# Two factors moved ahead of four transposes, and one difference moved behind two sums, on VectorE's queue in a two-layer graph attention kernel

## The chip, the cores and the metric

The kernel runs on one core of a Trainium2 chip. A core has TensorE (PE, matrix products into PSUM), VectorE (DVE), ScalarE (ACT), GpSimd (POOL, unused here but for some constants) and SyncE (SP), which issues all DMAs. Each engine works through its own queue of instructions and waits on semaphores for the others. The metric is the device time of one execution in microseconds (us), taken as the median of several runs.

## The reference

32 graphs ("elements") of 512 nodes with 512 features, and two layers, all in float32. Layer 0 is attention with 8 heads, in which the adjacency multiplies the exponentials, and a layer norm; layer 1 is a graph attention whose logits are a sum of two vectors:

```python
q, k, v = heads(x @ Wq.T + bq), heads(x @ Wk.T + bk), heads(x @ Wv.T + bv)
logits = einsum('bhqd,bhkd->bhqk', q, k) / sqrt(64) + log(clip(adj, 1e-8, None))
out = einsum('bhqk,bhkd->bhqd', softmax(logits), v) @ Wo.T + bo
x = layer_norm(x + out)
f = x @ fc_w.T + fc_b
m = (f @ q_w + q_b) + (f @ k_w + k_b).T + (1 - adj) * -1e9
out = softmax(leaky_relu(m)) @ f + x
```

## The kernel before

The elements go through a software pipeline written out by hand. For element b the kernel runs layer 0 of b beside layer 1 of element b - 2 and the joining work of element b - 1. The order of instructions on every engine is the order in which the Python functions issue them; no scheduler changes it. Elements 2 to 30 go through `first_two` (head pairs 0 and 1) and `second_two` (head pairs 2 and 3), thus 29 times. Elements 0 and 1 go through `slot`, and element 31 through `joining_slot` and `slot`. `joining_slot` has its own copy of the sequence that the change touches.

Products of 512 x 512 matrices are done as seven products of quarters with sums and differences (Strassen's scheme in Winograd's form). In layer 1 the product z = n^T e^T (n: the normalised features, e: the softmax weights) is done by `seven_z`. Its two operands are first made on VectorE. The weights of element b - 2 are "spread" by 16 DMAs of 64 KB (`spread_blocks`, L148) that are issued at the end of `second_two` of the element before; `eT` then turns them in place with four transposes of 32 x 32 blocks (L576). Sums and differences of quarters follow. The lines of `seven_z` that matter here, A for quarters of n, E for quarters of the turned weights:

```python
left = {1: A["11"], 2: A["12"], 3: A["12"], 4: A["22"], 5: s1, 6: A["11"], 7: A["21"]}
right = {1: E["11"], 2: E["21"], 3: E["22"], 4: E["21"], 5: t1, 6: E["11"], 7: E["12"]}
def before1():                             # extra[1]: L1073, L1074
    sub(t1, E["12"], E["11"])
    sub(A["21"], A["11"], A["21"])
def after0():                              # extra[2]: L1077, L1078
    sub(E["11"], E["22"], t1)
    sub(A["11"], s1, A["11"])
def after1():                              # extra[3]: L1081
    sub(E["12"], E["22"], E["12"])
```

`extra[0]` (L1070) forms s1, `extra[4]` (L1084, L1085) comes ahead of the fourth product, `extra[5]` (L1088) and `extra[6]` (L1091) add results. On TensorE `zs[0]` is products one and five (16 matmuls each), `zs[1]` six and two, `zs[2]` seven and three, `zs[3]` four. All run through the helper `halves` (L213) into three banks of PSUM, mx, my and mz, whose roles rotate from element to element. ScalarE copies results out (L1052, L1053, L1058, L1059, L1067). Product six reads what L1077 and L1078 write; both of these overwrite an operand of product one.

Ahead of z, `eight_scores` runs the scores of two head pairs (L852 on TensorE) and ScalarE's exponentials (L859, L861) into eight tiles `at`. `factor(b, p, kc)` (L887, VectorE) multiplies such a tile by the adjacency tile cT. The factored tiles are read by the value products (L913), which come on TensorE after z. `scaled` (L468) multiplies n by gamma for the residual, `turn_a` (L598) turns two rows of blocks of cT in place, and `divided` (L949 to L959) inverts sums that have come back through DRAM and sends the reciprocals by DMA to the tile R, which `scale` (L968) reads.

Of the kernel before, what the change touches and what calls it, by code (L numbers as in the profile page):

```python
# [30 lines left out]
def kernel(  # L31
# [280 lines left out]
    def transpose_units(src, dst, psum, evict, name):  # L312

        units = []
        for i in range(4):
            def unit(i=i):
                pt = psum.tile([P, 512], FP, tag="m", name=f"pt_{name}_{i}")
                for c in range(4):
                    nc.tensor.transpose(pt[:, ts(c, P)], src[:, c, ts(i, P)], ident)
                evict(dst[:, i, :], pt)  # L320
            units.append(unit)
        return units
# [144 lines left out]
    def scaled(s, cs):  # L467
        nc.vector.tensor_mul(s["yb"][:, cs, :], s["n"][:, cs, :], over(K["gamma"], cs))  # L468
# [39 lines left out]
    def fast(ctx):  # L508
# [43 lines left out]
        def load_n(b):  # L552
            s = S[b]
            if b > 0:
                tag = "xT" if b == B - 1 else "n"
                s["n"] = act.tile([P, NC, D], FP, tag=tag, name=f"n_{b}")
                load_b(s["n"], x[b])
# [16 lines left out]
        def transposes(dst, src):  # L574
            return [
                lambda c=c: nc.vector.transpose(dst[:, c, :], src[:, c, :]) for c in range(4)  # L576
            ]
# [18 lines left out]
        def turn_a(kcs):  # L596
            for kc in kcs:
                nc.vector.transpose(cT[:, kc, :], cT[:, kc, :])  # L598
# [230 lines left out]
        def long_banks(b):  # L829
            return lambda: [  # L830
                lone[i].rearrange("p (n f) -> p n f", n=KH) for i in (2, 0, 1)
            ]
# [51 lines left out]
        def factor(b, p, kc):  # L884

            at = S[b]["at", p, kc]
            nc.vector.scalar_tensor_tensor(  # L887
                at, cT[:, kc, :].unsqueeze(1).to_broadcast([P, 2, N]), ADJ_MIN, at,
                ALU.max, ALU.mult,
            )  # L890

        def both(b, p):
            run(values(b, p))
# [9 lines left out]
        def values(b, p):  # L903
            s = S[b]
            s.setdefault("oT", [None] * NPAIR)

            def part(half):
                if half == 0:
                    s["po", p] = ps_o.tile([P, N], FP, tag="po", name=f"po_{b}_{p}")
                for kc in (2 * half, 2 * half + 1):  # L910
                    for j in range(2):
                        h = 2 * p + j
                        nc.tensor.matmul(  # L913
                            s["po", p][j * DK : (j + 1) * DK, :],
                            s["v"][h // 4][:, kc, ts(h % 4, DK)],
                            s["at", p, kc][:, j, :],
                            start=(kc == 0), stop=(kc == NC - 1),
                        )
                if half == 1:
                    s["oT"][p] = act.tile([P, N], FP, tag="oT", name=f"oT_{b}_{p}", bufs=6)  # L920
                    nc.scalar.copy(s["oT"][p], s["po", p])  # L921
            return [lambda: part(0), lambda: part(1)]

        def divide(b, p):


            s = S[b]
            ps = lone[0]
            for h in range(4):
                nc.tensor.matmul(  # L930
                    ps[h * BL : (h + 1) * BL, :], ones[:, :BL], s["as", p + h // 2][:, h % 2, :],
                    start=True, stop=True,
                )
            s["R", p] = act.tile([P, 2, N], FP, tag="R", name=f"R_{b}_{p}")
            r = s["R", p][:, 0, :]
            nc.scalar.copy(r, ps)
            m = 4 * N // P
            d0 = dram.tile([4, N], FP, tag="d0", name=f"d0_{b}_{p}")
            nc.sync.dma_start(out=d0, in_=r.rearrange("(h r) n -> h r n", r=BL)[:, 0, :])
            c = small.tile([P, 2, m], FP, tag="c", name=f"c_{b}_{p}")  # L940
            nc.sync.dma_start(out=c[:, 0, :], in_=d0.rearrange("h (a m) -> (h a) m", m=m))
            s["c", p] = c

        def divided(b, p):
            s = S[b]
            c = s["c", p]
            m = 4 * N // P
            i = 2 * b + p // 2
            nc.vector.tensor_scalar(c[:, 1, :], c[:, 0, :], SUM_MAX, None, ALU.is_le)  # L949
            nc.vector.scalar_tensor_tensor(  # L950
                c[:, 1, :], c[:, 0, :], SUM_MIN, c[:, 1, :], ALU.is_ge, ALU.mult,
                accum_out=seen[:, i : i + 1],
            )
            nc.vector.reciprocal(c[:, 0, :], c[:, 0, :])
            d1 = dram.tile([P, m], FP, tag="d1", name=f"d1_{b}_{p}")
            nc.sync.dma_start(out=d1, in_=c[:, 0, :])
            d1 = d1.rearrange("(k j a) m -> j k (a m)", k=2, j=2)
            for j in range(2):
                nc.sync.dma_start(  # L959
                    out=s["R", p][j * DK : (j + 1) * DK, :, :],  # L960
                    in_=d1[j].unsqueeze(0).to_broadcast([DK, 2, N]),
                )

        def scale(b, p):
            s = S[b]
            for k in range(2):
                oT = s["oT"][p + k]
                nc.vector.tensor_mul(oT, oT, s["R", p][:, k, :])  # L968
# [127 lines left out]
        def eT(b):  # L1096
            s = S[b]
            if b >= B - 2:
                t = io.tile([P, NC, N], FP, tag="x", name=f"eT_{b}")
                s["eT"] = t.rearrange("p t (c n) -> p t c n", c=NC)  # L1100
                return transpose_units(s["e"], t, ps_m, nc.scalar.copy, f"e_{b}")
            s["eT"] = s["eP"].rearrange("p c (t n) -> p t c n", t=NC)
            return transposes(s["eP"], s["eP"])
# [46 lines left out]
        def new_yb(b):  # L1150
            S[b]["yb"] = act.tile([P, NC, D], FP, tag="yb", name=f"yb_{b}")
# [144 lines left out]
        def run(units):  # L1296
            for u in units:
                u()
# [173 lines left out]
        def eight_scores(b, ps):  # L1472

            n = 0
            for p in ps:
                for kc in range(NC):
                    score(b, p, kc, n % 3 == 0)
                    n += 1

        def first_two(b):  # L1480

            last, nxt = b - 1, b + 1
            if b == 2:
                run(values(last, 3))
                run(seven_qk(b, 1))
                scale(last, 0)
            divide(last, 2)
            eight_scores(b, (0, 1))  # L1490
            new_yb(b - 2)
            scaled(S[b - 2], slice(0, KH))
            zs, extra = seven_z(b - 2)
            extra[0]()
            run(eT(b - 2))
            extra[1]()
            extra[3]()
            factor(b, 0, 0)
            zs[0]()
            extra[2]()  # L1500
            factor(b, 0, 1)
            scaled(S[b - 2], slice(KH, NC))
            turn_a((2, 3))
            zs[1]()
            extra[4]()
            factor(b, 0, 2)
            zs[2]()
            extra[5]()
            divided(last, 2)
            factor(b, 0, 3)  # L1510
            zs[3]()
            extra[6]()
            load_n(last)
            load_x(nxt)
            factor(b, 1, 0)
            factor(b, 1, 1)
            factor(b, 1, 2)
            factor(b, 1, 3)
            first_difference(last, third)
            wos, wo_adds = seven_wo(last, long_banks(last))  # L1520
            wos[0]()
            both(b, 0)
            next_qk = seven_qk(b, 2)
            next_qk[0]()
            both(b, 1)
            run(sums_in_place(b, 0))
            scale(last, 2)
            first_sum(last)
            run(next_qk[1:4])
            run(sums_in_place(b, 1))  # L1530
            run(next_qk[4:])
            next_qk = seven_qk(b, 3)
            wos[1]()
            offset_rows(S[b - 2], slice(0, KH))
            run(wo_adds[0])
            wos[2]()
            wo_adds[1][0]()
            offset_rows(S[b - 2], slice(KH, NC))
            run(wo_adds[1][1:])
            wos[3]()  # L1540
            run(wo_adds[2])
            next_qk[0]()
            wos[4]()
            run(wo_adds[3])
            run(next_qk[1:4])
            run(stats_units(S[last], small, last))
            invert(S[b - 2])
            run(next_qk[4:])
# [367 lines left out]
```

## Time and profile before

| what | value |
|---|---|
| median of 3 runs | 3384.49 us (3382.42 to 3388.7) |
| profiled execution | 3383.92 us, its span 3382.1 us, granted TensorE clock 1.0 |
| TensorE busy | 3332.2 us (99%), 25914 matmuls |
| TensorE weight loads busy | 2032.1 us (60%) |
| VectorE busy | 3001.1 us (89%), 5313 instructions |
| ScalarE busy | 1408.8 us (42%) |
| one factor (L887) | 1214 ns, 468 of them |
| one transpose of eP (L576) | 680 ns, 120 of them, VectorE idle 72.4 us before them |
| mean share of the 16 DMA engines | 36% by the queue that SP issues to |

Times are counted from the start of the span. In a timeline line the first number is the start, the second how long it lasted, then the engine, the line of the kernel, the operation, the tile written and the tiles read; in brackets stands the time that the engine was idle before it and what ended that. The view of waits sums such idle times by who waited for whom. The ends of matmuls are modelled, since matmuls overlap; their starts are recorded. An element takes about 104 us.

### The profile page before, as it was taken

To read this page: it belongs to the slowest core of one execution; us is meant where nothing else is said; L and a number is where in the kernel's file an instruction comes from. 1 tells how busy PE (TensorE), PEld (TensorE's weight loads), DVE (VectorE), ACT (ScalarE), POOL (GpSimd) and SP (SyncE) were. 2 spreads that over 40 slices of the span, in tenths; PEclk is the share of its full clock that TensorE was granted. 3 is DMA by queue.
4 is the path that set the end of the run, shared out by engine and by line. 5 is a ranking of instruction groups with operands and counts; after the bars stand their busy time and mean duration, and the time that the engine had idled before them with its cause. 6 is when DMAs were issued, how large, how long until landed. Compare 5 with 4: busy or idle time off the path is not lost.

```text
span 3382.1 us, 64140 instructions
## 1 busy us (share of the span) xinstructions
PE 3332.2 (99%) x25914; PEld 2032.1 (60%) x25914; DVE 3001.1 (89%) x5313; ACT 1408.8 (42%) x2559; POOL 0.9 (0%) x9
## 2 busy tenths in 40 slices
PE   9999999999999999999999999999999999999999
PEld 4566666665666656666566666566665666656645
DVE  7889898898898998989989889888899898998988
ACT  3444434434434344334443343443434434344343
POOL 0000000000000000000000000000000000000000
PEclk9999999999999999999999999999999999999999
DMA  4334243342433433334424234343343333443321
GB/s 125 53 65 92 61 88 67 61 92 67 85 70 61 85 86 67 74 57 86 91 61 86 68 62 92 67 85 69 58 89 82 70 73 57 85 88 65 81 70 49
DMA packets 881654, 252.83 MB, mean 75 GB/s; under 512 B 806732, under 2 KB 809036, under 8 KB 881352
## 3 DMA queue, kind: packets, MB, share of 16 engines
q1 hardware_dynamic: 881352, 248.67, 36.1%
q8 instruction: 206, 3.38, 0.4%
q14 instruction: 96, 0.79, 0.1%
HBM read 182.46 MB, written 34.65 MB: 64 GB/s over the span
## 4 chain that ended last, share of the span: by engine, by line
PE 79%; DVE 13%; ACT 3%; DMA 2%; SPq 2%; issue 1%; DVEq 0%; ACTq 0%
PE f L213 20%; PE my L213 12%; PE mx L213 12%; PE mz L213 12%; PE po L913 11%; PE sc L852 5%; DVE at L887 3%; SPq L148 2%; DVE eP L576 2%; PE my L852 1%; DVE R L392 1%; DVE yb L801 1%; DMA d<-R 1%; PE mz L852 1%; PE mx L852 1%
## 5 line engine op out<-in xcount | busy, mean ns | idle before, releaser
L887 DVE SCALAR_TENSOR_TENSOR at<-cT,at 128x1024 f32<-128x1024 f32 x468 | 553.9, 1214 | 0.0
L913 PE MATMUL po<-at,v 128*64 128x512 f32 x2048 | 468.7, 594 | 2.0 <-DVE fold_more L298 1.6
L900 DVE TENSOR_TENSOR at<-at,at 128x1024 f32<-128x1024 f32 x348 | 423.8, 1218 | 8.0
L861 ACT ACTIVATE at<-sc 128x1024 f32<-128x1024 f32 x328 | 332.0, 1070 | 53.4 <-PE sc L852 53.4
L852 PE MATMUL sc<-qT,kT 64*128 64x512 f32 x1312 | 317.3, 593 | 0.4 <-ACT at L861 0.4
L913 PEld LDWEIGHTS po<-at,v 128*64 128x64 f32 x2048 | 156.5, 137 | 237.2 <-issue 154.2
L921 ACT COPY oT<-po 128x512 f32<-128x512 f32 x128 | 75.0, 586 | 480.4 <-PE po L913 480.4
L213 PE MATMUL f<-xT,wq 128*64 128x256 f32 x2032 | 265.8, 379 | 0.0
L213 PE MATMUL f<-T,qk_s 128*64 128x256 f32 x2032 | 254.8, 379 | 0.1
L852 PEld LDWEIGHTS sc<-qT,kT 64*128 64x128 f32 x1312 | 120.1, 186 | 165.7 <-ACT at L861 79.8
L213 PEld LDWEIGHTS f<-xT,wq 128*64 128x64 f32 x2032 | 159.5, 137 | 87.1 <-issue 34.3
L213 PEld LDWEIGHTS f<-T,qk_s 128*64 128x64 f32 x2032 | 159.4, 137 | 72.6 <-issue 14.9
L655 ACT COPY f<-f 128x256 f32<-128x256 f32 x127 | 45.3, 357 | 345.3 <-PE f L213 345.3
L661 ACT ACTIVATE qT<-f,bq 128x256 f32<-128x256 f32 x127 | 60.2, 474 | 217.7 <-PE f L213 217.7
L576 DVE STREAM_TRANSPOSE eP<-eP 128x512 f32<-128x512 f32 x120 | 74.7, 680 | 72.4 <-DMA d<-R 61.9
L852 PE MATMUL my<-qT,kT 64*128 64x512 f32 x254 | 133.5, 605 | 0.0
L213 PE MATMUL f<-xT,wk 128*64 128x256 f32 x1016 | 132.9, 379 | 0.0
L213 PE MATMUL f<-xT,qk_s 128*64 128x256 f32 x1016 | 132.9, 379 | 0.0
L213 PE MATMUL f<-T,wk 128*64 128x256 f32 x1016 | 132.9, 379 | 0.0
L852 PE MATMUL mz<-qT,kT 64*128 64x512 f32 x248 | 130.5, 606 | 0.0
L213 PE MATMUL my<-eP,n 128*64 128x256 f32 x960 | 116.0, 381 | 14.0 <-DVE n L1078 11.1
L213 PE MATMUL mz<-eP,n 128*64 128x256 f32 x960 | 116.0, 381 | 11.3 <-DVE n L1078 11.3
(430 smaller groups left out, 6400.3 us busy)
## 6 DMA issues: line engine op xcount, KB each, us to landing
cT<-in_adj_dram SPq DMA_DIRECT2D x512, 64.0 KB
R<-d SPq DMA_DIRECT2D x126, 256.0 KB
x<-in_x_dram SPq DMA_DIRECT2D x124, 256.0 KB
n<-in_x_dram SPq DMA_DIRECT2D x31, 1024.0 KB
L<-in_adj_dram SPq DMA_DIRECT2D x60, 512.0 KB
eP<-L SPq DMA_DIRECT2D x480, 64.0 KB
out_dram<-yb SPq DMA_DIRECT2D x58, 512.0 KB
w<-dk SPq DMA_DIRECT2D x32, 256.0 KB
```

Of the source, the lines that this page charges most:

```text
L148: nc.sync.dma_start(out=dst[j * BL : (j + 1) * BL, :, :].rearrange("r c (t q f) -> q r (c t) f", q=P // BL, f=BL)[i], in_=src[i * BL : (i ...
L213: nc.tensor.matmul(to[ts(h, DK)], left[:, ts(h, DK)], right, start=start, stop=stop, skip_group_check=True,)
L392: nc.vector.scalar_tensor_tensor(junk, s["n"][:, c, :], 1.0, u, ALU.mult, ALU.mult, accum_out=to[:, c : c + 1])
L576: lambda c=c: nc.vector.transpose(dst[:, c, :], src[:, c, :]) for c in range(4)
L655: nc.scalar.copy(ps["b"], ps["a"])
L661: nc.scalar.activation(q[:, H:], ps["a"], AF.Identity, bias=bq)
L852: nc.tensor.matmul(parts[j], s["kT", p][rows, ts(kc, P)], s["qT", p][rows, :], start=True, stop=True,)
L861: nc.scalar.activation(at, sc, AF.Exp, scale=SCALE)
L887: nc.vector.scalar_tensor_tensor(at, cT[:, kc, :].unsqueeze(1).to_broadcast([P, 2, N]), ADJ_MIN, at, ALU.max, ALU.mult,)
L900: lambda kc=kc: nc.vector.tensor_add(to, to, s["at", p, kc]) for kc in range(1, NC)
L913: nc.tensor.matmul(s["po", p][j * DK : (j + 1) * DK, :], s["v"][h // 4][:, kc, ts(h % 4, DK)], s["at", p, kc][:, j, :], start=(kc == 0), s ...
L921: nc.scalar.copy(s["oT"][p], s["po", p])
```

## The change

In `first_two` the calls are put in another order; nothing else is edited:

```diff
             zs, extra = seven_z(b - 2)
             extra[0]()
+            factor(b, 0, 0)
+            factor(b, 0, 1)
             run(eT(b - 2))
             extra[1]()
-            extra[3]()
-            factor(b, 0, 0)
             zs[0]()
             extra[2]()
-            factor(b, 0, 1)
+            extra[3]()
             scaled(S[b - 2], slice(KH, NC))
             turn_a((2, 3))
             zs[1]()
```

On VectorE's queue the two L887 of the first two tiles of head pair 0 stand ahead of the four L576, where they stood behind L1081 and behind L1078. L1081 stands behind L1078, where it stood behind L1074. The queues of TensorE, ScalarE and SyncE have the same instructions in the same order; on TensorE the first matmul of product seven now also waits for VectorE (for L1081), and L887 and L1077 wait on their own engine's earlier results as well.

## Prediction

> **What bounds the kernel now.** I read the page's busy shares first, then TensorE's waits, then VectorE's waits, then the timeline of one element around the moved lines.
>
> The busy shares, with TensorE (PE) at 99%:
>
> ```profile
> PE 3332.2 (99%) x25914; PEld 2032.1 (60%) x25914; DVE 3001.1 (89%) x5313; ACT 1408.8 (42%) x2559; POOL 0.9 (0%) x9
> ```
>
> TensorE sets the end, so an edit on VectorE (DVE) can only pay where TensorE waits for VectorE. The view of TensorE's waits (us in total, times, longest) shows one such place:
>
> ```profile
> PE mz L213 <- DVE n L1078: 11.3, 10, 1.6
> PE my L213 <- DVE n L1078: 11.1, 9, 1.6
> PE mx L213 <- DVE n L1078: 7.7, 7, 1.6
> PE my L592 <- DMA n<-in_x_dram: 4.5, 2, 3.7
> ```
>
> The three lines are one wait under the names of three rotating banks: 30.1 us in 26 waits for L1078, the second operand of z's sixth product. Nothing else reaches 5 us. VectorE has the matching gap a little earlier:
>
> ```profile
> DVE eP L576 <- DMA d<-R: 61.9, 26, 3.4
> ...
> DVE eP L576 <- DMA eP<-L: 10.4, 4, 3.0
> ...
> DVE n L1084 <- PE mx L213: 3.7, 10, 0.4
> ```
>
> It stands idle 72.3 us in all (about 2.4 us an element) ahead of the transposes of the spread weights, until transfers land. Later it waits for TensorE at L1084. The timeline of one element shows both (start, duration, idle before in brackets):
>
> ```profile
> 1137.76 2.49 DVE L576 STREAM_TRANSPOSE eP<-eP 128x512 f32<-128x512 f32 x4 [2.17 <-DMA d<-R]
> 1140.13 1.95 PE L213 MATMUL mx<-eP,n 128*64 128x256 f32 x16
> 1140.28 0.69 DVE L1073 TENSOR_TENSOR R<-eP 128x512 f32<-128x512 f32 x1
> 1141.49 0.69 DVE L1081 TENSOR_TENSOR eP<-eP 128x512 f32<-128x512 f32 x1
> 1141.91 1.90 PE L213 MATMUL my<-R,third 128*64 128x256 f32 x16
> 1142.09 1.22 DVE L887 SCALAR_TENSOR_TENSOR at<-cT,at 128x1024 f32<-128x1024 f32 x1
> 1142.18 0.57 ACT L1052 COPY mz<-mx 128x512 f32<-128x512 f32 x1 [0.35 <-PE mx L213]
> 1143.23 0.68 DVE L1077 TENSOR_TENSOR eP<-eP,R 128x512 f32<-128x512 f32 x1
> 1143.83 0.68 DVE L1078 TENSOR_TENSOR n<-third,n 128x512 f32<-128x512 f32 x1
> 1144.66 1.95 PE L213 MATMUL mx<-eP,n 128*64 128x256 f32 x16 [0.86 <-DVE n L1078]
> 1148.37 0.69 DVE L1084 TENSOR_TENSOR n<-n 128x512 f32<-128x512 f32 x1 [0.37 <-PE mz L213]
> ```
>
> VectorE is idle from 1135.59, transposes, forms two differences, then does L1081 (needed only by the seventh product) and a factor of L887 (needed only by the value products some 10 us later), and only then L1077 and L1078. TensorE starts product one at 1140.13, five at 1141.91, and six not before 1144.66.
>
> **What the Trainium skill says.** "Perfetto Trace Analysis", section "Identifying the Most-Contended Engine", says that matmul busy time overstates how near TensorE is to its limit. The trace agrees: 99% busy beside 60% of weight loads. So I measure TensorE by starts of products, not by busy time. The same page, "Per-engine timelines", says that a VectorE record ends with the write's acknowledgement, after the point from which the next instruction may begin. The trace agrees: L1077 lasts 0.68 us but L1078 starts 0.60 after it, so I add starts, not durations. "DMA: Bandwidth & Descriptors", "Rules for kernel authors", advises to do compute and wait late on a transfer's semaphore; the idle 2.17 us above is what is lost otherwise. "TensorE: Matmul & The Clock Gate", "Step-by-step: what each phase is for", says that only weight loads are pulled ahead and matmuls keep program order. The trace agrees in that nothing of the later products appears before 1144.66.
>
> **The change, part by part.** No instruction is added or removed. On VectorE two factors go ahead of the transposes and L1081 goes behind L1078, in 29 elements (the joining slot keeps the old order). TensorE, ScalarE and the DMA queue keep their order; none of the moved instructions issues a DMA, and none is moved past one.
>
> *The two factors ahead.* Start to start one takes 1.14 us (1142.09 to 1143.23), so the pair takes 2.28, and the transposes can start 2.2 us after the point where VectorE now goes idle. Their inputs must be there: in this element the exponentials of the first two scores end 0.30 us before that point and 0.62 us after it, and the factors would start at -0.08 and 1.06. What hides them is the wait for the transfers, which ends 1.45 to 3.42 us after that point (median 2.4). In 10 elements of 29 it ends before 2.2 us, and the factors hold the transposes up, by 0.75 us at most. That costs nothing: product one needs the first two transposes, 1.3 us after the start of the four, thus at 3.5, and it starts at about 4.5 behind the scores. Without that cover each 1 us would cost 1 us.
>
> *One factor and L1081 out of the way of L1077.* From the transposes' start to L1077 it is 5.47 us now (1137.76 to 1143.23). Without the factor (1.14) and L1081 (0.60) it is 3.73. Counted from 1135.59: 2.20 + 3.73 = 5.93 at the soonest, where the transfers landed at 2.17.
>
> *A wait that comes to the front.* L1077 overwrites an operand of product one, so it cannot start before that product is done. Today it comes so late that this never shows. How long after product one's modelled end, at 6.49, L1077 is released is not in the trace; the bounds are 0.03 (L1084 after its product) and 0.10 (ScalarE's L1052, 1142.18 against 1142.08). So L1077 starts at 6.52 to 6.59, not at 7.64. Behind it on VectorE are L1078, L1081, the second half of `scaled` and two transposes of cT; TensorE waits for L1078 alone. L1078 ends 1.28 us after L1077's start, and product six starts 0.14 us later: 7.94 to 8.01.
>
> *TensorE's own pace.* Products follow each other in 1.73 to 1.78 us where nothing is waited for (1140.13 to 1141.91, then 1144.66 to 1146.41), and product five starts at 6.32, so six can start at 8.07 to 8.14 on TensorE's side (1.75 to 1.82). That is now the later of the two, instead of 9.07: 0.93 to 1.0 us in this element.
>
> *L1081 later.* It ends at about 8.4; product seven starts some 3.5 us after product six, at 11.6. Free; if it were late, seven would wait.
>
> *The sum.* I took this rule (six at the later of five plus 1.75 to 1.82 and L1078 plus 0.14, with each element's own landing) through all 29 elements. From product one to product six they take 139.8 us together now (mean 4.82, from 3.60 to 5.55), and 103.6 to 105.4 after. Saving 34.3 to 36.1; I take 35.3.
>
> *Is it kept to the end?* The trace answers this, because the delay already varies. From product six's start to the next element's product one it is 99.37 us (within 0.02) in 24 of 29 elements, however late six was. The first element is nearly what the change would make of all: its transfers landed at 1.45, and six starts 3.60 us after one:
>
> ```profile
> 202.48 1.95 PE L213 MATMUL mx<-eP,n 128*64 128x256 f32 x16
> 204.26 1.90 PE L213 MATMUL my<-R,third 128*64 128x256 f32 x16
> 206.08 1.95 PE L213 MATMUL mx<-eP,n 128*64 128x256 f32 x16
> ```
>
> The next element's product one starts at 305.44, thus 99.36 later. VectorE meets TensorE again at L1084, 3.71 us after product six, in all 30 elements; after the change it will get there about 1.1 us early and wait there instead. The stall therefore goes from TensorE's path to VectorE's slack.
>
> Profiled execution: 3383.92 us (span 3382.1 and 1.8 around it). 3383.92 - 35.3 = 3348.6; the median of the runs is 0.6 above the profiled one, so 3349.
>
> **Rivals.** *A: the gain stays in part.* Work later in the element is timed from before the moved lines: L949 needs sums whose transfer was issued at 1137.59, and the reciprocals come back by DMA for L968. If one of these became late, half could go: 3384.5 - 17.6 = 3367. Against: L949 comes 13.7 us after that issue and neither line shows idle time; the constant 99.37. For: the transfers' landing sets the transposes in 19 elements, and each 1 us later than about 2.9 us costs 1 us.
>
> *B: slower.* L1077 is released by the end of product five (about 8.24), not of product one, if its wait stands on a later instruction of TensorE than the data need. Then L1077 starts at 8.27, six at 9.69, against a mean of 9.34 now: 0.35 x 29 = 10 us, so 3395. It decides against the change as soon as L1077's release is later than 7.91, its mean start now. Against: in the first element L1077 ran at 204.65 while product five ran until 206.16:
>
> ```profile
> 204.65 0.69 DVE L1077 TENSOR_TENSOR eP<-eP,R 128x512 f32<-128x512 f32 x1
> ```
>
> *C: nothing moves.* The wait for L1078 is an artefact of modelled ends and TensorE is at its pace anyway: 3384. Against: the 99.37 above; starts, not ends, show the delay.
>
> **How the numbers follow.** Chances: main case 0.89 (3349), A 0.05 (3367), B 0.03 (3395), C 0.03 (3384). The main case's own bounds are 3384.5 - 36.1 = 3348.4 and 3384.5 - 34.3 = 3350.2; the runs before spread 2.1 below and 4.2 above their median, and a slower release of L1077 by 0.1 us would cost up to 2.9 more. That gives 3346 to 3357; I add 1 below for products that follow at 1.73. The main case lies in it about 9 times in 10, so the range holds the time some 8 times in 10. 0.2% (6.8 us) is about what a measurement of this kernel can tell from no change. Faster: main case and A, 0.94; within 0.2%: C, 0.03; slower: B, 0.03.
>
> **What would show it.** TensorE's waits for L1078 fall from 30.1 to under 4 us; VectorE's idle time ahead of the eP transposes falls from 72.3 to about 11; L1084's idle rises from 0.37 to about 1.1 us an element; product one to six takes 3.5 to 3.85 us; 99.37 stays. I am wrong if L1077 starts more than 0.25 us after product one's end, if 99.37 grows, or if the transfers land later against the scores.

## The result and the profile after

The changed kernel takes 3347.59 us (median of 5 runs, 3345.6 to 3348.87) against 3384.49 before (5 runs, 3381.73 to 3388.7): the ratio is 0.9888, 95% interval 0.9873 to 0.9902. That is 36.9 us less, and 1.4 us below the 3349 of the prediction. The profiled executions, 3345.6 and 3383.92, differ by 38.3 us.

On the page of the changed kernel these are the busy shares, and by engine the chain of work that ended last (followed back from the last instruction, each time to what released it):

```profile
PE 3326.2 (99%) x25914; PEld 1929.8 (58%) x25914; DVE 3001.7 (90%) x5313; ACT 1407.5 (42%) x2559; POOL 0.9 (0%) x9
...
PE 97%; DVE 2%; ACT 1%; DMA 0%; issue 0%; SPq 0%; DVEq 0%; ACTq 0%
```

The busy times of TensorE, VectorE and ScalarE are within 0.2% of before, since the work is the same. What changed is the chain. Before it was:

```profile
PE 79%; DVE 13%; ACT 3%; DMA 2%; SPq 2%; issue 1%; DVEq 0%; ACTq 0%
```

VectorE and the DMAs have almost gone from it, and TensorE has 97%. The view of TensorE's waits has only one line for L1078 left:

```profile
...
PE my L213 <- DVE eP L576: 1.7, 2, 1.5
...
PE my L213 <- DVE n L1078: 0.6, 1, 0.6
```

The wait for L1078 was 30.1 us. What remains of it is the joining slot, which was not edited. The line above it is product one waiting for the transposes, 1.5 us of it in the joining slot too. VectorE's waits, in us, times and the longest:

```profile
...
DVE eP L576 <- DMA d<-R: 9.8, 15, 1.9
DVE n L1084 <- PE mz L213: 9.3, 10, 0.9
DVE n L1084 <- PE my L213: 9.3, 10, 0.9
DVE n L1084 <- PE mx L213: 8.7, 10, 0.9
...
DVE eP L1077 <- PE mx L213: 2.3, 6, 0.7
```

VectorE's idle time ahead of the transposes, 72.3 us before, is 12.3 in all. It turns up in part where it costs nothing: L1084 waits 27.2 us in its 30 instances, against 11.1 before. These lines of the timeline (others between them are left out) show the same element as in the prediction:

```profile
1123.80 2.36 DVE L887 SCALAR_TENSOR_TENSOR at<-cT,at 128x1024 f32<-128x1024 f32 x2
1126.28 2.49 DVE L576 STREAM_TRANSPOSE eP<-eP 128x512 f32<-128x512 f32 x4
1128.44 1.95 PE L213 MATMUL mx<-eP,n 128*64 128x256 f32 x16
1130.22 1.90 PE L213 MATMUL my<-R,third 128*64 128x256 f32 x16
1130.43 0.69 DVE L1077 TENSOR_TENSOR eP<-eP,R 128x512 f32<-128x512 f32 x1 [0.33 <-PE mx L213]
1131.04 0.68 DVE L1078 TENSOR_TENSOR n<-third,n 128x512 f32<-128x512 f32 x1
1131.94 1.90 PE L213 MATMUL mx<-eP,n 128*64 128x256 f32 x16
1135.61 0.69 DVE L1084 TENSOR_TENSOR n<-n 128x512 f32<-128x512 f32 x1 [0.93 <-PE mz L213]
```

Read it beside the earlier one: product one to product five 1.78 us as before, but five to six 1.72 us where it was 2.75. Product six no longer shows a gap ahead of it, and L1077 is idle 0.33 us for product one.

From the starts of all 29 elements: product one to six takes 3.56 us in the mean (4.82 before), and from six to the next element's product one 99.34 (99.37 before).

### The profile page after: what moved, and what is told of

The parts are those of the page before. It is cut to its first block, busy times and chain, and to the rows that moved or that the text cites. A ratio compares the mean times of both kernels' runs of the same rounds, so it can differ in the third digit from the quotient of the medians.

```text
span 3343.8 us, 64256 instructions
## 1 busy us (share of the span) xinstructions
PE 3326.2 (99%) x25914; PEld 1929.8 (58%) x25914; DVE 3001.7 (90%) x5313; ACT 1407.5 (42%) x2559; POOL 0.9 (0%) x9
## 4 chain that ended last, share of the span: by engine, by line
PE 97%; DVE 2%; ACT 1%; DMA 0%; issue 0%; SPq 0%; DVEq 0%; ACTq 0%
PE f L213 22%; PE mx L213 15%; PE my L213 15%; PE mz L213 15%; PE po L913 13%; PE sc L852 8%; PE my L852 2%; PE mx L852 2%; PE mz L852 2%; PE mx L930 1%; PE my L930 1%; PE mz L930 1%; PE mz L490 0%; PE my L326 0%; DVE at L869 0%
## 5 line engine op out<-in xcount | busy, mean ns | idle before, releaser
L887 DVE SCALAR_TENSOR_TENSOR at<-cT,at 128x1024 f32<-128x1024 f32 x468 | 551.7, 1216 | 0.0
L913 PEld LDWEIGHTS po<-at,v 128*64 128x64 f32 x2048 | 146.4, 137 | 247.4 <-issue 160.9
L213 PEld LDWEIGHTS f<-xT,wq 128*64 128x64 f32 x2032 | 149.5, 137 | 97.1 <-issue 35.6
L213 PEld LDWEIGHTS f<-T,qk_s 128*64 128x64 f32 x2032 | 149.4, 137 | 82.6 <-issue 16.1
L852 PE MATMUL mx<-qT,kT 64*128 64x512 f32 x234 | 123.2, 606 | 0.0
L213 PE MATMUL mx<-eP,n 128*64 128x256 f32 x960 | 114.6, 380 | 0.5 <-DVE eP L576 0.5
```

Of the source, the lines that this page charges most:

```text
L213: nc.tensor.matmul(to[ts(h, DK)], left[:, ts(h, DK)], right, start=start, stop=stop, skip_group_check=True,)
L852: nc.tensor.matmul(parts[j], s["kT", p][rows, ts(kc, P)], s["qT", p][rows, :], start=True, stop=True,)
L887: nc.vector.scalar_tensor_tensor(at, cT[:, kc, :].unsqueeze(1).to_broadcast([P, 2, N]), ADJ_MIN, at, ALU.max, ALU.mult,)
L913: nc.tensor.matmul(s["po", p][j * DK : (j + 1) * DK, :], s["v"][h // 4][:, kc, ts(h % 4, DK)], s["at", p, kc][:, j, :], start=(kc == 0), s ...
```

## The experiments

Theory 1 says that the way from the transposes to L1078 is what counts, and that the factors ahead only find free room. Theory 2 says that what counts is that VectorE's idle wait is filled with work. Each kernel below differs from the kernel before or from the changed one only in the order of calls in `first_two`; the last one differs in `joining_slot` too. All are timed beside the kernel before, and each saving is counted from the time that it had there (medians of 3382.39, 3383.13 and 3383.79 us). The times from product to product are means over the 29 elements, unless another thing is said. A line of three dots stands for lines left out.

**Both factors ahead, L1081 left in its place** (diff against the kernel before):

```diff
             extra[0]()
+            factor(b, 0, 0)
+            factor(b, 0, 1)
             run(eT(b - 2))
             extra[1]()
             extra[3]()
-            factor(b, 0, 0)
             zs[0]()
             extra[2]()
-            factor(b, 0, 1)
```

> Both factors ahead of the transposes, L1081 left in its old place between them and L1077. Theory 1 (the way from the transposes to L1078 is what counts): one of the two removed pieces, 0.60 us, comes back. From transposes to L1077 it is 4.33 us instead of 3.73, which shows only where the transposes start later than 2.2 us after L1070, since L1077 waits for product one until 6.54 anyway. With the landings of the trace before, 28 to 30 us are saved: 3355. Theory 2 (what counts is that the idle wait for the transfers is filled with two factors): the same saving as the change, 3348.

Measured: 3353.79 us, ratio 0.9913 (0.9899 to 0.9926), so 28.6 us saved. Product one to six takes 3.85 us. TensorE's waits for L1078 in this kernel:

```profile
...
PE my L213 <- DVE n L1078: 2.8, 7, 0.6
PE mz L213 <- DVE n L1078: 1.7, 5, 0.5
...
PE mx L213 <- DVE n L1078: 1.2, 3, 0.5
```

This is 5.7 us in 15 waits. One is the joining slot's; most of the others are in elements whose transposes start more than 2.5 us after L1070. Theory 1 expected 29.5 us of saving and theory 2 36.5, so theory 1 has the number. L1081 has its share in the change, though it makes only 0.29 us an element here (3.85 against 3.56), since product one and TensorE's own pace hide the rest.

**L1081 behind L1078, both factors left** (against the kernel before):

```diff
             extra[1]()
-            extra[3]()
             factor(b, 0, 0)
             zs[0]()
             extra[2]()
+            extra[3]()
             factor(b, 0, 1)
```

> L1081 behind L1078, both factors in their old places. Theory 1: the way from the transposes to L1077 gets 0.60 us shorter in every element (4.87 instead of 5.47), nothing else changes; product six is late by 0.6 us less in 28 of 29 elements: about 17 us saved, 3367. L1077 then still starts without a wait for product one in most elements. Theory 2: no wait is filled, so nothing is saved, 3384.

Measured: 3363.52 us, ratio 0.9943 (0.993 to 0.9957), 18.9 us saved; product one to six 4.22 us, 0.60 less than before. This is the length of L1081, start to start, and 0.60 x 29 is 17.4 us. Theory 2 (no saving) fails here.

**Nothing ahead, everything behind L1078** (against the kernel before):

```diff
             run(eT(b - 2))
             extra[1]()
-            extra[3]()
-            factor(b, 0, 0)
             zs[0]()
             extra[2]()
+            extra[3]()
+            factor(b, 0, 0)
             factor(b, 0, 1)
```

> Nothing ahead of the transposes; both factors and L1081 behind L1078. Theory 1: VectorE idles 2.3 us ahead of the transposes as before, but from transposes to L1077 it is 3.73 us, so product six starts as in the change: 36 us saved, 3348. VectorE reaches L1084 some 1.2 us later than in the change's order with no wait there, which the waits further on (L778) take up. Theory 2: no wait is filled, so the gain is gone: 3384, or 3367 for L1081 alone.

Measured: 3375.57 us, ratio 0.998 (0.9972 to 0.9988). Only 6.8 us are saved, so theory 1 as stated fails too. Its first half came true: product one to six takes 3.54 us, as in the changed kernel. But from six to the next product one it is now 100.42 us instead of 99.34. The timelines of TensorE and of VectorE show where, in the second of the 29 elements:

```profile
308.80 1.90 PE L213 MATMUL mz<-eP,n 128*64 128x256 f32 x16
...
312.26 1.90 PE L213 MATMUL mz<-eP,n 128*64 128x256 f32 x16
314.44 1.95 PE L213 MATMUL mx<-eP,n 128*64 128x256 f32 x16 [0.28 <-DVE n L1084]
316.77 1.95 PE L213 MATMUL mz<-eP,n 128*64 128x256 f32 x16 [0.39 <-DVE L L1088]
```

```profile
309.11 2.35 DVE L887 SCALAR_TENSOR_TENSOR at<-cT,at 128x1024 f32<-128x1024 f32 x2
...
313.74 0.64 DVE L1084 TENSOR_TENSOR n<-n 128x512 f32<-128x512 f32 x1
...
316.04 0.68 DVE L1088 TENSOR_TENSOR L<-mz,L 128x512 f32<-128x512 f32 x1
```

Product six starts at 308.80. Product three reads what L1084 writes (the description above names only product four with `extra[4]`) and starts 5.64 us after product six, where it is 5.18 in the changed kernel. Product four overwrites the bank that L1088 reads and starts 7.97 us after product six instead of 6.91. L1084 starts 4.94 us after product six; in the changed kernel it is 3.67. The two factors behind L1078 do not lengthen the way to product six, but they lengthen the way to products three and four, and 1.08 us x 29 = 31 us are given back there.

**Only the second factor ahead** (against the kernel before):

```diff
             extra[0]()
+            factor(b, 0, 1)
             run(eT(b - 2))
...
             extra[2]()
-            factor(b, 0, 1)
```

> Only the second factor goes ahead of the transposes, out of its old place behind L1078; the first factor and L1081 stay between the transposes and L1077. Theory 1: half of the wait is filled, but nothing on the way to product six gets shorter: 0 us, 3384, with VectorE idle 1.1 us less ahead of the transposes and more at L1084. Theory 2: half of the factors' gain, 12 to 18 us: about 3370.

Measured: 3382.26 us against 3382.39, ratio 1.0003 (0.9995 to 1.0011). VectorE's idle time ahead of the transposes falls from 72.4 to 22.0 us, and L1084's rises from 11.1 to 44.1. Filling 50 us of the wait is worth nothing by itself: the idle time only moves. Theory 2 (about 3370) fails again.

After these four I changed theory 1 into 1a: several dates count, not one (L1078 for product six, L1084 and L1088 for products three and four), and VectorE's work may stand anywhere that keeps them all. Theory 2a says instead that VectorE has no room for the factors but the idle wait.

**A third piece ahead** (against the changed kernel):

```diff
             factor(b, 0, 1)
+            scaled(S[b - 2], slice(KH, NC))
             run(eT(b - 2))
...
             extra[3]()
-            scaled(S[b - 2], slice(KH, NC))
             turn_a((2, 3))
```

> The changed kernel with a third piece ahead of the transposes, the second half of scaled (1.14 us). The transposes can start 3.34 us after L1070 at the soonest, about 0.9 us after most landings. By the rule of the prediction (transposes to L1077 3.73 us, L1077 to product six 1.42 us) product six starts some 8.5 us after L1070 instead of 8.05: 0.42 us x 29 = 12 us over the changed kernel, 3360. If the room ahead of the transposes were set by something else than the landings and product one's start, nothing would be lost: 3348.

Measured: 3357.07 us, ratio 0.9927 (0.9913 to 0.994): 26.1 us less than before, where the change alone had 36.9. The transposes start 3.34 us after the end of L1070 in the mean (3.32 to 3.50) and product six at 8.50, as expected.

**Two more pieces ahead** (against the changed kernel; `turn_a((2, 3))` goes ahead with the half of `scaled`):

```diff
             factor(b, 0, 1)
+            scaled(S[b - 2], slice(KH, NC))
+            turn_a((2, 3))
             run(eT(b - 2))
...
             extra[3]()
-            scaled(S[b - 2], slice(KH, NC))
-            turn_a((2, 3))
```

> The changed kernel with the second half of scaled and the two transposes of cT ahead of the transposes of the spread weights (1.14 and 1.22 us). They can start 4.56 us after L1070 at the soonest; product one waits for them till 5.9, and product six starts at 9.7 instead of 8.05: 1.63 us x 29 = 47 us over the changed kernel, 3395, slower than the kernel before by some 11 us. From the kernel with scaled ahead to this one each further us ahead should cost a full us in every element.

Measured: 3390.84 us, ratio 1.0027 (1.0017 to 1.0037), slower than before. The transposes start at 4.55 and product six at 9.67. From the kernel above, 1.21 us of later transposes cost 33.8 us, or 1.16 us in each of 29 elements. The new wait, in the view of TensorE's waits:

```profile
PE mz L213 <- DVE eP L576: 12.8, 10, 1.6
PE mx L213 <- DVE eP L576: 12.6, 10, 1.6
PE my L213 <- DVE eP L576: 11.2, 9, 1.2
```

In these two kernels product six follows the start of the transposes by 5.16 and 5.12 us. In most elements of the changed kernel it starts 8.05 us after L1070. So the transposes may start up to about 2.9 us after L1070 before product six is late (an estimate: 8.05 - 5.16); the prediction had worked out the same 2.9. The change uses 2.2 of it.

**The factors still further back** (against the changed kernel):

```diff
-            factor(b, 0, 0)
-            factor(b, 0, 1)
             run(eT(b - 2))
...
             extra[4]()
-            factor(b, 0, 2)
+            factor(b, 0, 0)
             zs[2]()
             extra[5]()
             divided(last, 2)
-            factor(b, 0, 3)
+            factor(b, 0, 1)
             zs[3]()
             extra[6]()
+            factor(b, 0, 2)
+            factor(b, 0, 3)
```

> Nothing ahead of the transposes; L1081 behind L1078; the two factors go still further back, behind L1085 and L1088, and the next two factors behind L1091. The kernel with all behind L1078 kept product six on time but held products three and four up, since L1084 and L1088 came 1.26 us later. Theory 1a (two dates count, L1078 for product six and L1088 for product four, and the factors may stand anywhere that keeps both): L1084 and L1088 come as in the changed kernel, and what may be late is the last of the four factors for the value products, by about 0.2 us: 3348 to 3355. Theory 2a (VectorE has no room for the factors but the idle wait): the 1.1 us an element appears again further on: about 3376.

Measured: 3385.5 us, ratio 1.0004 (0.9998 to 1.0011). Theory 1a's number fails, and theory 2a's 3376 is also too low. The seven products run as in the changed kernel (product one to six 3.53 us, product four 6.91 after six), and the value products start at 8.63 as there. Behind the first of them TensorE is 0.13 us later than in the changed kernel, about what theory 1a allowed for late factors. The main loss is further on:

```profile
PE mx L213 <- DVE oT L774: 11.2, 10, 1.1
PE mz L213 <- DVE oT L774: 11.2, 10, 1.1
PE my L213 <- DVE oT L774: 10.1, 9, 1.1
```

This is a wait that neither kernel had: L774 forms an operand of layer 0's output product, some 28 us after product six. Counted from product four, TensorE starts the product that needs it 1.41 us later than in the changed kernel. From six to the next product one it is 100.74 us. There is thus one more date than I had counted. On the way from L1088 to L774 VectorE is idle only 0.2 us, in both kernels, so nearly all of the two factors' 2.28 us arrives there: L774 starts 2.26 us later.

**Only the first factor ahead** (against the changed kernel):

```diff
             factor(b, 0, 0)
-            factor(b, 0, 1)
             run(eT(b - 2))
...
             extra[3]()
+            factor(b, 0, 1)
             scaled(S[b - 2], slice(KH, NC))
```

> The changed kernel with only the first factor ahead of the transposes; the second stays behind L1078 and L1081, about where it was. Theory 1a: L1084 starts 1.14 us sooner than in the kernel with both behind, about 3.8 us after product six, and L1088 ends at about 6.8, just in time for product four at 6.9: no loss, 3348. So the move of the second factor would bring nothing by itself. Theory 2a: half of what filling the wait brings is lost, about 14 us: 3362.

Measured: 3343.59 us against 3383.13, ratio 0.9885 (0.987 to 0.99). The whole saving, 39.5 us, is there with one factor ahead, and theory 2a's 3362 fails. L1084 starts 3.80 us after product six and L1088 ends at 6.78, both as expected; product four starts at 6.91. So VectorE can have one factor, 1.14 us, behind the sums at no cost, but not two: its idle time ahead of L1084 is 0.01 us here, where the changed kernel has 0.9.

**The changed kernel again, and one factor ahead with the joining slot**, on one chip. The second has the order of the kernel just above and, in `joining_slot`:

```diff
             extra[1]()
-            extra[3]()
             zs[0]()
             extra[2]()
+            extra[3]()
```

> The changed kernel itself, beside the next one on the same chip: 36 to 39 us under the kernel before, ratio 0.988 to 0.989. Product one to six 3.56 us in the mean, product six to the next product one 99.33.

> One factor ahead, the second behind L1078 and L1081, and the joining slot's L1081 behind L1078 too. If VectorE can be about 1.1 us later behind the sums at no cost, the second factor's place does not matter: the same time as the changed kernel beside it. The joining slot happens once; its wait for L1078 is 0.55 us, so at most that is gained, which a measurement cannot tell from nothing. If the second factor's move had its own worth, this kernel would be slower than the changed one by 10 us or more.

Measured: 3345.51 us, ratio 0.9884 (0.9867 to 0.99), and 3343.94 us, ratio 0.9882 (0.9865 to 0.9898). Product one to six takes 3.57 us in the first and 3.54 in the second, and from six to the next product one it is 99.36 and 99.32. The two are the same within what can be told; 10 us of difference is excluded. In the second the joining slot's wait for L1078 is gone (the gap ahead of product six is 0.00 instead of 0.55).

## Why the prediction was right, and where its reasons were short

*The wait that was to go.* Right, and its size: product one to six was to fall from 139.8 us in all to 103.6 to 105.4, and fell to 103.2. The small rest is TensorE's pace: products follow at 1.73 us in most elements, under the 1.75 to 1.82 that I allowed. With 1.73 the rule of the prediction gives 103.1 from the landings before. This term gave 36.6 us instead of 35.3. On the way from the transposes to L1077 the kernels with L1081 alone and the factors alone split it as the working did: 0.60 us for L1081 (4.87 instead of 5.47) and 1.13 for the first factor (4.34). In the time from product one to six they give 0.60 and 0.97, together more than the 1.26 of the change: with both moved, product one and TensorE's pace come to the front.

*The wait that comes to the front.* Right. L1077 starts 0.05 us after product one's modelled end in 21 of 29 elements, inside the bounds of 0.03 to 0.10. Rival B (release by product five) is excluded by that. In six elements it starts more than 0.25 us after, which the prediction named as a sign of being wrong. There the cause is not the release: the transposes start 2.85 us or more after L1070, since the transfers land late, and L1077 comes behind them without a wait.

*The room for the factors.* Right, and the bound with it. The kernels with more ahead cost nearly what the rule said: 26.1 us saved for the 24 expected of one more piece, and 7.7 us slower than before for the 11 expected of two more. The elements whose transfers land late (the transposes start up to 3.76 us after L1070) still take up to 3.81 us from product one to six, within the 3.5 to 3.85 foretold.

*The constant 99.37.* It holds but for 0.05 us: 99.32 in 17 of 29 elements. The starts on TensorE show where the 0.05 comes from. Where product six had to wait (all 29 elements before, 7 after), product two follows it by 1.749 us and the first matmul of L930 follows product four by 32.896. In the 22 elements without that wait it is 1.727 and 32.867. The last section says what differs. Over 29 elements the mean change of 0.04 us makes 1.1 us. With 36.6 that is 37.7 of the 38.3 us between the profiled executions; rival A did not occur.

*L1084.* Foretold idle about 1.1 us an element, measured 0.9. A sum of the known pieces gives this: 0.37 of before, 1.14 for the second factor that left the place behind L1078, less 0.60 for L1081 that came into it, makes 0.91 (an estimate).

*The total.* The median came out 1.4 us below the 3349 foretold, which is in part luck. The profiled executions differ by 38.3 us, 3.0 more than the 35.3 foretold, but the profiled execution after is the fastest of its five and lies 2.0 us under their median.

What was short is the reason given for the order behind the sums. The prediction said of what stands behind L1077 that "TensorE waits for L1078 alone". For product six that is so. The kernel with everything behind L1078 showed that it is not so for VectorE's queue as a whole: products three and four wait for L1084 and L1088, and further on L774 has a date as well. In the change these dates are kept because the factors went into the idle wait; had both only gone behind L1078, most of the gain would have been lost. The prediction also did not say that the second factor's move brings nothing, though its sum credits only the first factor and L1081. The second one's move is worth nothing, ahead by itself (3382.26 against 3382.39) or left out (3343.59): VectorE has about 1.1 us to spare behind the sums, which is one factor, and two factors behind them cost 1.1 us at products three and four.

One remark of the prediction goes further than its source: the Trainium skill's "Perfetto Trace Analysis", section "Identifying the Most-Contended Engine", says only that the matmul busy share is no good measure; that it overstates is my reading of the 99% beside 60%.

The views name a small transfer (d<-R) for most of the waits ahead of the transposes. The trace of the kernel before also has the times at which the semaphores were raised, and these point to another releaser: in 28 of 29 elements the transposes start 0.31 to 0.32 us after the last raise by the last of the 16 spreading transfers (0.67 us in the other). The last raise by d<-R lies 0.14 to 0.20 us ahead of them in 23 elements and 0.5 to 1.3 us in five, and in one element it comes 0.04 us after they have started. So the view names the transfer that came nearest in time, and the wait is for the spreading transfer. Both were left as they are in every kernel, so this rests on the times and not on an experiment.

## What to carry to other kernels

Where a busy engine waits for another one, list every date that the other engine has to keep until the next point where it idles, not only the wait that the profile shows; a step moved back out of one wait can miss the next date. Filling an idle wait and shortening the way to the awaited step are two things. Here the second factor put into the wait gave 0. The shortest way to product six, got by moving both factors and L1081 back, gave only 6.8 us, as the next dates were missed. With the first factor in the wait and the rest moved back all dates were kept, and the saving was 39.5 us, no less than the 36.9 of the change. If the trace has the delay varying by itself from element to element, compare the time from the delayed step to the next repeat: if it is constant, as 99.37 us was here, what is saved at that step can be expected to be kept to the end, as long as the other engine keeps its later dates.

## What the runs showed of the hardware that was not expected

TensorE's weight loads are 5% less busy after the change (1929.8 against 2032.1 us) with the same 25914 instructions. The single records are not shorter: one load of the projections takes 137 ns and one matmul 379 ns in both. What differs is how they lie. The matmuls come in pairs, and pairs follow each other in 216 ns in both kernels. The second of a pair mostly starts either 6 to 7 or about 36 ns after the first. Before, 408 of 759 groups of eight matmuls of the projections have the 36 ns in their usual record (1.06 us instead of 1.03); after, about 100 have it. With 7 ns the records of loads overlap more, and their busy time is less.

The starts show when this changes. In all 29 elements before, and in the 7 after in which product six had to wait, the first pair of product six is 7 ns apart and the later ones 36. Before, in the element shown, this lasts through all groups until L930, some 40 us later, where it is 7 ns again. In the 22 elements after without the wait it stays at 7. Such a wait thus cost 0.02 us more behind product six and 0.03 at L930, which are the 0.05 us above. Why the pairs keep the longer distance no run shows. For the reader of a profile it means that weight-load busy time can change by 5% with no change of the work.
